# A graph network of two layers: transposes of x and the edges' counts moved to the end of the period ahead

## The chip, the cores and the metric

The kernel runs on one core of a Trainium2 chip. The metric is the device time of one execution in microseconds (us). A core has five engines with a queue each: TensorE (PE; its weight loads are listed apart as PEld), VectorE (DVE), ScalarE (ACT), GpSimd (POOL) and SyncE (SP), which here only issues DMA transfers. An engine takes its instructions in the order of the program, so an instruction that waits holds up all that stand behind it on the same engine.

## The reference

128 independent graphs of 128 nodes with 512 features in fp32. Each goes through a graph attention layer with 8 heads, a residual and a layer norm, and then through a hypergraph layer with a hidden width of 1024, again with residual and norm. Cut to what is computed:

```python
# layer 0
feats = einsum('bnf,hfu->bhnu', X, W)                    # 8 heads of 64
dense = leaky_relu(e_self[..., :, None] + e_neigh[..., None, :], 0.2) + NEG_BIG * (1 - A)
out = relu(einsum('bhij,bhju->bhiu', softmax(dense), feats) + b)
x = layernorm(x + out)
# layer 1
H = (adj != 0)
Dn = 1 / einsum('nce,ne->nc', H, adj[:, 0, :])           # 0 where the sum is not positive
Be = 1 / H.sum(axis=1)                                   # the edges' counts
conv(x, W, b) = Dn * (H @ (Be * (H.T @ (x @ W.T)))) + b
h = layer_norm(relu(conv(x, W1, b1))) * gamma + beta
y = conv(h, W2, b2)
x = layernorm(x + y)
```

## The kernel before

The graphs go two by two: a pair `p` has two graphs `g`, and there are 64 pairs. The work on one pair is spread over five periods of a software pipeline, so that in one period the stages of several pairs stand side by side. Every step is registered with a lag (in which period after the pair's own) and a time within the period. All steps of all pairs are sorted by `(p + lag) * T + time`, and the program is written in that order. The times only set the order on each engine; what an instruction waits for is data.

```python
    def at(lag, time, fn, *args, since=0, until=PAIRS):
        steps.append((lag, time, fn.__name__, range(since, until), fn, args))
# ... cut
    T = 38.6
# ... cut
            time += (p + lag) * T
            todo.append((first.get((name, p) + args, first.get((name, p), time)), run, (fn, p, args)))
    with tc.manual_schedule():
        for _, fn, args in sorted(todo, key=lambda e: e[0]):
            fn(*args)
```

The steps that the change touches. The rows of `x` are loaded a second time in blocks (`xb`), so that VectorE's 32x32 transposes give the whole transpose `xT`; the first layer's features are products of `xT` and of GpSimd's sums `xS` of its parts. The rows of `adj` are loaded in blocks (`ab`) too; their transpose gives `hT`, and its row sums the counts `deg`. `x_transpose`, `edges` and the loads:

```python
    def x_transpose(p, s, g):
        if g == 0:
            s["xT"] = work.tile([P, 2, KF, N], F32, tag="xT", name=f"xT_{p}")
        nc.vector.transpose(
            s["xT"][:, g].rearrange("p k (b n) -> p k b n", b=NB),
            s["xb"][:, g * NB:(g + 1) * NB].rearrange("p b (f k) -> p k b f", k=KF),
        )
    at(1, 4.7, x_transpose, 0, since=2)
    at(1, 5.3, x_transpose, 1, since=2)
# ... cut
    @step(1, 3.4)
    def edges(p, s):
        # ... cut: deg, hT
            nc.vector.transpose(hT.rearrange("p g (b n) -> p (g b) n", b=NB), s["ab"])
        for g in range(2):
            nc.vector.tensor_scalar(
                hT[:, g, :], src[:, g, :], 0.0, None, op0=ALU.not_equal, op1=ALU.add,
                accum_out=deg[:, g:g + 1],
            )
        nc.vector.tensor_scalar(deg, deg, 1.0, None, op0=ALU.max)
        nc.vector.reciprocal(deg, deg)
# ... cut
    @step(1, 10.8)   # scale_edges, VectorE: hB = hT * deg
    @step(1, 34.7)   # propagator, TensorE: pd = hB, hT
    @step(1, 35.8)   # r_evict, VectorE: R = pd * dnb
# ... cut: per pair
            todo.append((16.2 if p == 2 else p * T + 19.0, load_blocks, (p,)))
            todo.append((p * T + 28.5, load_edges, (p,)))
```

All of `xb`, `ab`, `xT` and `hT` have one buffer. Between the attention and the hidden layer stand, for the pair of lag 2, in the second half of the period:

```python
    # attended (VectorE): y = pav / row sums;  add_bias (GpSimd): y + b0
    at(2, 22.5, attended, 0)
    at(2, 27.9, attended, 1)
    at(2, 24.1, add_bias, 0)
    at(2, 29.2, add_bias, 1)
    def residual(p, s, g):
        y = s["y"][:, g, :]
        nc.vector.scalar_tensor_tensor(y, y, 0.0, s["x"][:, g, :], op0=ALU.max, op1=ALU.add)
        moments(p, s, "a", y, g)              # bn_stats, bn_aggr on VectorE
    at(2, 26.2, residual, 0)
    at(2, 30.7, residual, 1)
    at(2, 30.8, rstds, "a")                   # VectorE: + eps; GpSimd: power -0.5 -> rsa
    # ScalarE at 33.12 .. 33.14: sh = -mean * rsa, then y = y * rsa + sh
# ... cut
    at(3, 0.0, propagate, 0)                  # TensorE: pz from y and R
    at(3, 1.1, z_evict, 0)                    # ScalarE: zT = pz
    # hidden: products phX, phY, phW from zT and from GpSimd's sums zS; h_sum (VectorE), relu (ScalarE)
```

`masked` (GpSimd: `nb` + `neg`), `leaky` (ScalarE) and `largest` (VectorE: `nm`) of the pair of lag 1 stand around the period's end, and ScalarE's `leaky` of three half heads stands between `y` and `zT`. Attention's transposes `eT` (VectorE) stand ahead of the products `pav`, and the layer norm of the output `o` ahead of them.

The second layer's product with `W2` is a chain of seven products `pyX`, `pyY`, `pyW` in TensorE. VectorE adds two of them at a time to `y2`; a column more in the product, 1/DH times ones, carries the mean of `h`. Its deviation comes from the squares of `h`, which ScalarE forms and GpSimd folds, TensorE transposes (`pm`) and VectorE sums:

```python
        nc.scalar.activation(
            s["sq"][:, g, q * KH // 2:(q + 1) * KH // 2, :], hid(s, g, q), AF.Square
        )
# ... cut
    at(3, 31.3, y_sum, 0, 0, 0, "Y", until=LAST)
    at(3, 33.9, y_sum, 1, 1, 2, "W", until=LAST)
    at(4, 0.1, y_sum, 0, 1, 1, "W", until=LAST)
# ... cut
    @step(3, 36.0, until=LAST)
    def h_rstd(p, s):
        m2 = small.tile([P, 2], F32, tag="m2", name=f"m2_{p}")
        for g, m in enumerate((s["y2"][:, 0, 0, QU:], s["py", 1][:, QU:QU + 1])):
            nc.vector.tensor_tensor(m2[:, g:g + 1], m, m, op=ALU.mult)
        ve = small.tile([P, 2], F32, tag="ve", name=f"veh_{p}")
        nc.vector.tensor_reduce(
            ve, s["pm"][:, :2 * N].rearrange("p (g f) -> p g f", g=2), AX.X, ALU.add
        )
        nc.vector.scalar_tensor_tensor(
            ve, ve, 1.0 / DH, m2, op0=ALU.mult, op1=ALU.subtract
        )
        nc.vector.tensor_scalar(ve, ve, 0.0, EPS, op0=ALU.max, op1=ALU.add)
        s["rs", "h"] = small.tile([P, 2], F32, tag="rs", name=f"rsh_{p}")
        nc.gpsimd.tensor_tensor(s["rs", "h"], ve, mhalf, op=ALU.pow)
    # y_scale (VectorE, lag 4, 0.6 and 1.3): y2 * rsh + bw;  output (TensorE, 10.9): pq
```

`s["py", 1]` is a copy in SBUF that ScalarE makes of a product; `y2` lies in SBUF too.

Of the kernel before, what the change touches and what calls it, by code (L numbers as in the profile page):

```python
# [8 lines left out]
F32 = mybir.dt.float32  # L9
AF = mybir.ActivationFunctionType  # L10
ALU = mybir.AluOpType
AX = mybir.AxisListType

EPS = 1e-5
# [6 lines left out]
def kernel(  # L21
# [45 lines left out]
    nc = tc.nc  # L67
    G, N, F = x.shape
    P = 128
    DH = w1t.shape[1]  # L70
# [3 lines left out]
    KH = DH // P  # L74
    HALF = 512
    QU = HALF // 2
# [8 lines left out]
    small = ctx.enter_context(tc.tile_pool(name="small", bufs=4))  # L85
# [212 lines left out]
    LAST = PAIRS - 1  # L298
    steps = []

    def step(lag, time, since=0, until=PAIRS):

        def keep(fn):
            steps.append((lag, time, fn.__name__, range(since, until), fn, ()))
            return fn
        return keep

    def at(lag, time, fn, *args, since=0, until=PAIRS):
        steps.append((lag, time, fn.__name__, range(since, until), fn, args))
# [62 lines left out]
            s["xb"][:, g * NB:(g + 1) * NB].rearrange("p b (f k) -> p k b f", k=KF),  # L372
        )

    at(1, 4.7, x_transpose, 0, since=2)
    at(1, 5.3, x_transpose, 1, since=2)

    def x_transpose_first(p, s):
        s["px"] = [bank(f"px_{p}_{g}") for g in range(2)]
# [14 lines left out]
        for g in range(2):  # L394
            nc.tensor.transpose(s["pt"][:, g * N:(g + 1) * N], s["a"][:, g, :], ident)

    @step(1, 3.4)
    def edges(p, s):

        deg = small.tile([P, 2], F32, tag="deg", name=f"deg_{p}")  # L400
        hT = work.tile([P, 2, N], F32, tag="hT", name=f"hT_{p}")
        if p < 2:
            src = s["pt"][:, :2 * N].rearrange("p (g n) -> p g n", g=2)
        else:
            src = hT
# [8 lines that stand above are left out]
        s["hT"], s["be"] = hT, deg  # L414
# [65 lines left out]
    def feature(s, i, to, start):  # L480
# [4 lines left out]
          feature, FW, since=2)  # L485
# [315 lines left out]
    def hid(s, g, q):  # L801
        return s["h"][:, g, q * KH // 2:(q + 1) * KH // 2, :]
# [26 lines left out]
    def square(p, s, g, q):  # L829
        if (g, q) == (0, 0):  # L830
            s["sq"] = work.tile([P, 2, KH, N], F32, tag="sq", name=f"sq_{p}")
        nc.scalar.activation(
            s["sq"][:, g, q * KH // 2:(q + 1) * KH // 2, :], hid(s, g, q), AF.Square
        )

    for (g, q), t in (((0, 0), 13.5), ((0, 1), 15.9), ((1, 0), 19.4), ((1, 1), 21.2)):
        at(3, t, square, g, q)
# [21 lines left out]
    def weigh(s, i, to, start):  # L859
# [3 lines left out]
          QU, 1, until=LAST)  # L863
# [9 lines left out]
        else:  # L873
            nc.vector.tensor_tensor(dst, s["py", i][:, :n], s["py", where][:, :n], op=ALU.add)

    at(3, 31.3, y_sum, 0, 0, 0, "Y", until=LAST)
    at(3, 33.9, y_sum, 1, 1, 2, "W", until=LAST)
    at(4, 0.1, y_sum, 0, 1, 1, "W", until=LAST)
    at(3, 37.2, y_sum, 1, 0, None, "X", until=LAST)
# [2 lines left out]
    def sum_squares(p, s):  # L882
        s["pm"] = bank(f"pm_{p}")
        for g in range(2):
            nc.tensor.transpose(s["pm"][:, g * N:(g + 1) * N], s["sq"][:, g, 0, :], ident)

    @step(3, 36.0, until=LAST)
    def h_rstd(p, s):
        m2 = small.tile([P, 2], F32, tag="m2", name=f"m2_{p}")
        for g, m in enumerate((s["y2"][:, 0, 0, QU:], s["py", 1][:, QU:QU + 1])):  # L890
            nc.vector.tensor_tensor(m2[:, g:g + 1], m, m, op=ALU.mult)
        ve = small.tile([P, 2], F32, tag="ve", name=f"veh_{p}")
        nc.vector.tensor_reduce(
            ve, s["pm"][:, :2 * N].rearrange("p (g f) -> p g f", g=2), AX.X, ALU.add
        )
        nc.vector.scalar_tensor_tensor(
            ve, ve, 1.0 / DH, m2, op0=ALU.mult, op1=ALU.subtract
        )
        nc.vector.tensor_scalar(ve, ve, 0.0, EPS, op0=ALU.max, op1=ALU.add)
        s["rs", "h"] = small.tile([P, 2], F32, tag="rs", name=f"rsh_{p}")  # L900
        nc.gpsimd.tensor_tensor(s["rs", "h"], ve, mhalf, op=ALU.pow)

# [64 lines left out]
    def last_rstd(p, s, g, v):  # L967
        ve = small.tile([P, 1], F32, tag="ve", name=f"ve_{g}")
        nc.vector.tensor_scalar(ve, v, 0.0, EPS, op0=ALU.max, op1=ALU.add)
        rs = small.tile([P, 1], F32, tag="rs", name=f"rs_{g}")  # L970
        nc.gpsimd.tensor_tensor(rs, ve, mhalf[:, :1], op=ALU.pow)
        return rs

    def last_h_rstd(p, s, g):
        m = s["py", g, 0][:, QU:QU + 1]
        m2 = small.tile([P, 1], F32, tag="m2", name=f"m2_{g}")
        nc.scalar.activation(m2, m, AF.Square)
        v = small.tile([P, 1], F32, tag="vl", name=f"vl_{g}", bufs=2)
        nc.vector.tensor_reduce(v, s["pm", g][:, :N], AX.X, ALU.add)
        nc.vector.scalar_tensor_tensor(v, v, 1.0 / DH, m2, op0=ALU.mult, op1=ALU.subtract)  # L980
        s["rs", "h", g] = last_rstd(p, s, g, v)

    def last_scale(p, s, g, j):
# [37 lines left out]
    for t, fn, *args in (  # L1021
        (8.0, last_weights),
        (24.2, last_weigh, 0, 0), (27.8, last_weigh, 0, 1), (31.3, last_sum_squares, 0),
        (31.4, last_h_rstd, 0), (31.5, last_weigh, 1, 0), (32.5, last_scale, 0, 0),
        (32.6, last_scale, 0, 1), (34.9, last_sum_squares, 1), (35.0, last_h_rstd, 1),
        (35.1, last_output, 0, 0), (35.2, last_output, 0, 1), (35.3, last_weigh, 1, 1, (0,)),
        (35.5, last_o_sum, 0, 0), (35.6, last_scale, 1, 0), (36.0, last_o_sum, 0, 1),
        (36.5, last_o_rstd, 0), (37.0, last_output, 1, 0), (37.1, last_weigh, 1, 1, (1,)),
        (37.2, last_o_sum, 1, 0), (38.7, last_scale, 1, 1), (38.75, last_norm, 0),
        (38.9, last_output, 1, 1), (39.6, last_o_sum, 1, 1), (40.0, last_o_rstd, 1),  # L1030
        (40.5, last_norm, 1),
    ):
        at(3, t, fn, *args, since=LAST)


    T = 38.6
    todo = [
        (11.1, prepare_first, (0,)), (12.0, prepare_first, (1,)), (15.45, prepare_first_sums, ()),
        (12.1, load_weights, (nc.scalar, w2_blocks, w2t, DH // 2, QU)),
        (13.05, prepare_vectors, ()),  # L1040
        (14.05, load_weights, (nc.scalar, w1_blocks[:2], w1t, F // 2, HALF)),
        (12.95, load_first_row, (1,)),
        (15.46, load_weights, (nc.sync, w1_blocks[:1:-1], w1t, F // 2, HALF)),
        (16.1, everywhere, (b2_bc, b2, nc.sync)),
        (79.0, prepare_hidden, (nc.gpsimd, 2)), (79.1, prepare_hidden, (nc.gpsimd, 0)),
# [14 lines left out]
    first = {  # L1060
        ("spread_rows", 0): 13.5, ("neighbours", 0): 14.0,
        ("nodes", 0): 12.9, ("write_nodes", 0): 12.92, ("spread_nodes", 0): 15.9,
        ("edges", 0): 14.46, ("scale_edges", 0): 14.47, ("propagator", 0): 14.55,
        ("r_evict", 0): 99.76,
        ("spread_rows", 1): 15.72, ("nodes", 1): 15.55, ("write_nodes", 1): 15.85,
        ("edges", 1): 110.4, ("scale_edges", 1): 110.5, ("neighbours", 1): 80.1,
# [25 lines left out]
    for p in range(PAIRS):  # L1092
        if p > 1:
            todo.append(({2: 79.5, 3: 143.1}.get(p, p * T), load, (p,)))
            todo.append((16.2 if p == 2 else p * T + 19.0, load_blocks, (p,)))
            todo.append((p * T + 28.5, load_edges, (p,)))
        for lag, time, name, pairs, fn, args in steps:
            if p not in pairs:
                continue
            if p == 0 and lag == 2 and time < 8.5:  # L1100
                time *= 0.2
            if p == LAST:

                time = {
                    ("attend", 0): 24.25, ("attended", 0): 25.5, ("add_bias", 0): 25.6,
                    ("attend", 1): 25.95, ("attended", 1): 26.0, ("add_bias", 1): 26.1,
                    ("residual", 1): 26.3, ("rstds", "a"): 26.4,
                }.get((name,) + args[:1], time)
            if p == LAST - 1:
                time = {  # L1110
                    ("product", 2): 24.22 if (lag, time) > (3, 20.0) else time,
                    ("product", 5): 29.5 if (lag, time) > (3, 20.0) else time,
                    ("squares", 0): 26.5, ("squares", 1): 26.6, ("h_sums", 2): 22.3,
                    ("sum_squares",): 43.0, ("h_rstd",): 43.2, ("y_scale", 1): 5.8, ("y_scale", 0): 5.9,
                }.get((name,) + args[:1], time)
            time += (p + lag) * T
            todo.append((
                first.get((name, p) + args, first.get((name, p), time)), run, (fn, p, args)
            ))
# [46 lines left out]
```

## Time and profile before

| | before |
|---|---|
| time, median of 3 runs | 2584.59 us (2584.38 to 2586.65) |
| profiled run: span | 2570.0 us |
| TensorE matmul / weight loads busy | 2530.1 us (98%) / 2266.9 us (88%) |
| VectorE busy | 2114.2 us (82%) |
| GpSimd busy | 1753.4 us (68%) |
| ScalarE busy | 1535.0 us (60%) |
| TensorE clock granted | 0.997 |
| HBM traffic | 133 GB/s over the span |

A row of the profile's list in order of time reads: start in us, duration in us, engine, line of the kernel, operation, output and inputs by the program's names, shape, number of instructions merged; in brackets the idle time of the engine just before it, and the work whose end released it. A row of merged instructions has the sum, from the first start to the last end. On TensorE a weight load of the next product overlaps the matmul that runs.

### The profile page before, as it was taken

How to read it: one execution, taken by the hardware profiler on the slowest of the kernel's cores; microseconds unless marked ns; L12 is line 12 of the kernel's file. 1: busy time of each engine (PE TensorE's matmuls, PEld its weight loads, DVE VectorE, ACT ScalarE, POOL GpSimd, SP SyncE). 2: the span in 40 equal slices, each digit the busy share in tenths (PEclk: the TensorE clock that was granted, in tenths of full speed). 3: DMA queues.
4: the chain of work that ended last, by engine and by line, in shares of the span. 5: the costliest groups of instructions: out<-in, count | busy, mean ns of one | idle time of the engine just before them, and what ended most of it. 6: DMA issues, size and time to landing. Idle time of an engine off the chain costs nothing.

```text
span 2570.0 us, 48486 instructions
## 1 busy us (share of the span) xinstructions
PE 2530.1 (98%) x16349; PEld 2266.9 (88%) x16349; DVE 2114.2 (82%) x4584; ACT 1535.0 (60%) x4481; POOL 1753.4 (68%) x1806
## 2 busy tenths in 40 slices
PE   7999999999999999999999999999999999999998
PEld 5898988898888888989988889889888888898897
DVE  7887888878878878788888788787887888888875
ACT  4565665655755656557556566565565665655653
POOL 5767767676676676766766767667667666676674
PEclk9999999999999999999999999999999999999999
DMA  6444444444444444444454444444444444444431
GB/s 184 133 137 133 136 139 140 130 128 141 131 133 133 140 140 130 129 143 130 133 143 138 133 133 140 138 130 131 137 136 133 133 140 140 129 130 142 131 121 52
DMA packets 420840, 343.75 MB, mean 134 GB/s; under 512 B 141272, under 2 KB 370160, under 8 KB 420592
## 3 DMA queue, kind: packets, MB, share of 16 engines
q1 hardware_dynamic: 417120, 336.19, 44.2%
q10 hardware_dynamic: 3472, 4.47, 0.6%
q8 instruction: 130, 2.13, 0.3%
q14 instruction: 118, 0.97, 0.1%
HBM read 238.83 MB, written 101.71 MB: 133 GB/s over the span
## 4 chain that ended last, share of the span: by engine, by line
PE 83%; DVE 7%; DMA 4%; issue 2%; ACT 2%; POOL 1%; SPq 1%; DVEq 0%; POOLq 0%; ACTq 0%
PE phX L792 14%; PE pyX L473 14%; PE pfX L473 9%; PE phW L792 8%; PE pav L662 8%; PE pyW L473 7%; PE pfW L473 4%; PE pz L757 4%; PE phY L792 4%; PE pq L915 3%; PE pyY L473 3%; PE pfY L473 2%; DMA dnb<-dd_d 2%; ACT nb L592 1%; DVE o L745 1%
## 5 line engine op out<-in xcount | busy, mean ns | idle before, releaser
L329 ACT COPY py<-pyX 128x257 f32<-128x257 f32 x189 | 70.6, 374 | 539.4 <-PE pyX L473 526.3
L792 PEld LDWEIGHTS phX<-zS,w_sb 128*128 128x128 f32 x3072 | 363.1, 192 | 32.9 <-issue 29.3
L792 PE MATMUL phX<-zS,w_sb 128*128 128x128 f32 x3072 | 374.4, 275 | 2.1 <-POOL xS L455 1.3
L843 POOL TENSOR_TENSOR sq<-sq 128x512 f32<-128x512 f32 (+2 forms) x384 | 342.4, 892 | 20.2
L606 ACT ACTIVATE nb<-nb,nm 128x128 f32<-128x128 f32 x1024 | 324.5, 392 | 18.4 <-DVE nm L598 18.4
L576 POOL TENSOR_TENSOR nb<-nb,neg 128x512 f32<-128x512 f32 x256 | 317.8, 1273 | 14.3 <-DMA nb<-rd 14.3
L592 ACT ACTIVATE nb<-nb,ft 128x128 f32<-128x128 f32 x1020 | 317.3, 389 | 7.1 <-POOL nb L576 7.1
L822 ACT ACTIVATE h<-h,vecs 128x128 f32<-128x128 f32 x768 | 245.1, 392 | 88.3 <-DVE h L807 88.3
L693 DVE SCALAR_TENSOR_TENSOR y<-y,x 128x512 f32<-128x512 f32 x128 | 153.5, 1199 | 167.6 <-POOL y L686 167.6
L662 PEld LDWEIGHTS pav<-ft,eT 128*128 128x128 f32 x2048 | 243.5, 192 | 30.9 <-PE pfX L473 20.8
L709 POOL TENSOR_TENSOR rso<-veo,mhalf 128x2 f32<-128x2 f32 x63 | 44.1, 700 | 332.1 <-DVE veo L707 326.9
L662 PE MATMUL pav<-ft,eT 128*128 128x65 f32 x2048 | 246.8, 274 | 5.0
L473 PE MATMUL pyX<-w_sb,hS 128*128 128x257 f32 x1008 | 242.5, 382 | 0.0
L473 PE MATMUL pyX<-w_sb,h 128*128 128x257 f32 x1008 | 239.5, 379 | 0.5 <-ACT py L329 0.5
L473 PE MATMUL pyW<-w_sb,hS 128*128 128x256 f32 x1008 | 238.5, 378 | 0.0
L473 PEld LDWEIGHTS pyW<-w_sb,hS 128*128 128x128 f32 x1008 | 190.7, 189 | 27.4
L455 POOL TENSOR_TENSOR xS<-xT 128x256 f32<-128x256 f32 x124 | 117.9, 951 | 140.4 <-DVE xT L370 138.7
L473 PEld LDWEIGHTS pyX<-w_sb,h 128*128 128x128 f32 x1008 | 186.3, 190 | 25.5 <-ACT py L329 0.9
L473 PEld LDWEIGHTS pyX<-w_sb,hS 128*128 128x128 f32 x1008 | 186.2, 190 | 24.3
L686 POOL TENSOR_TENSOR y<-y,b_bc 128x512 f32<-128x512 f32 x128 | 162.4, 1269 | 62.9 <-DVE y L677 62.9
L598 DVE TENSOR_REDUCE nm<-nb 128x4 f32<-128x512 f32 x256 | 168.0, 676 | 2.9 <-ACT nb L592 2.2
L627 DVE STREAM_TRANSPOSE eT<-eb 128x512 f32<-128x512 f32 x252 | 161.9, 678 | 0.0
(167 smaller groups left out, 5865.1 us busy)
## 6 DMA issues: line engine op xcount, KB each, us to landing
nb<-rd SPq DMA_DIRECT2D x127, 512.0 KB, 6.3
ed<-nb SPq DMA_DIRECT2D x126, 512.0 KB, 2.6
eb<-ed SPq DMA_DIRECT2D x504, 128.0 KB, 2.9
x<-in_x_dram SPq DMA_DIRECT2D x64, 512.0 KB, 7.2
out_dram<-o SPq DMA_DIRECT2D x63, 512.0 KB, 2.8
xb<-in_x_dram SPq DMA_DIRECT2D x248, 128.0 KB, 3.0
a<-in_adj_dram SPq DMA_DIRECT2D x64, 128.0 KB, 6.5
w<-in_adj_dram SPq DMA_DIRECT2D x128, 64.0 KB, 4.3
```

The source lines that it names most:

```text
L473: nc.tensor.matmul(to[:, :n], lhs[:, k, :], rhs[:, k, :n], start=bool(start) and k == 0, stop=(k == nk - 1), skip_group_check=True,)
L576: nc.gpsimd.tensor_tensor(t, t, neg[:, :, None, :].to_broadcast([P, NB, HH, B]), op=ALU.add)
L592: nc.scalar.activation(t, t, AF.Prelu, bias=s["ft"][:, g, h, 0:1], alpha=SLOPE)
L598: nc.vector.tensor_reduce(s["nm"][:, g, hs], scores(p, s, g, hs).rearrange("p b h j -> p h b j"), AX.XY, ALU.max, negate=True,)
L606: nc.scalar.activation(t, t, AF.Exp, bias=s["nm"][:, g, h:h + 1])
L627: nc.vector.transpose(s["eT"][:, g, hs, :].rearrange("p h (b i) -> p h b i", b=NB), s["eb", g][:, :, hs, :].rearrange("p b h j -> p h b j"),)
L662: nc.tensor.matmul(t[:, h * (U + 1):(h + 1) * (U + 1)], s["eT"][:, g, q * HH + h, :], s["ft"][:, g, q * HH + h, 2:], start=True, stop=True,)
L686: nc.gpsimd.tensor_tensor(s["y"][:, g, :], s["y"][:, g, :], b0_bc, op=ALU.add)
L693: nc.vector.scalar_tensor_tensor(y, y, 0.0, s["x"][:, g, :], op0=ALU.max, op1=ALU.add)
L792: nc.tensor.matmul(to[:, m * N:(m + 1) * N], w[:, k, m * P:(m + 1) * P], rhs[:, k, :], start=bool(start) and m == 0 and k == 0, stop=(k == ...
L822: nc.scalar.activation(dst[:, k, :], src[:, k, :], AF.Relu, bias=b1_sb[:, c:c + 1])
L843: nc.gpsimd.tensor_tensor(t[:, :n, :], t[:, :n, :], t[:, n:2 * n, :], op=ALU.add)
```

## The change

VectorE's work is moved in the period and partly given to GpSimd.

- The two transposes of `x` are done 17 us sooner, in the second half of the pair's own period instead of early in the next one: one ahead of the first residual, one ahead of the second.
- The edges' transpose and counts are done at the end of the pair's own period, ahead of `R`. Their rows are loaded at 20.5 instead of 28.5, behind the blocks of `x`.
- The deviation of `h`: the squares of the two means are formed by GpSimd in a step of its own (`h_means`), and the subtraction, the floor at 0 and the epsilon by GpSimd as well. VectorE keeps the sum over `pm`. ScalarE's squares take the factor 1/DH with them, as a scale of DH^-0.5.
- The sum of `pyY` stands at 30.6 instead of 31.3, ahead of `h_means`, which reads its mean column.

It is meant to keep VectorE's queue short in the first part of a period and to use idle time in the second. Cut: the last pair's own deviation, which drops its factor 1/DH, and the starting times of pair 2.

```diff
-    at(1, 4.7, x_transpose, 0, since=2)
-    at(1, 5.3, x_transpose, 1, since=2)
+    at(0, 26.15, x_transpose, 0, since=2)
+    at(0, 30.65, x_transpose, 1, since=2)
...
-    @step(1, 3.4)
+    @step(0, 35.75)
     def edges(p, s):
...
         nc.scalar.activation(
-            s["sq"][:, g, q * KH // 2:(q + 1) * KH // 2, :], hid(s, g, q), AF.Square
+            s["sq"][:, g, q * KH // 2:(q + 1) * KH // 2, :], hid(s, g, q), AF.Square,
+            scale=DH ** -0.5,
         )
...
-    at(3, 31.3, y_sum, 0, 0, 0, "Y", until=LAST)
+    at(3, 30.6, y_sum, 0, 0, 0, "Y", until=LAST)
...
+    @step(3, 30.62, until=LAST)
+    def h_means(p, s):
+
+        s["m2"] = small.tile([P, 2], F32, tag="m2", name=f"m2_{p}")
+        for g, m in enumerate((s["y2"][:, 0, 0, QU:], s["py", 1][:, QU:QU + 1])):
+            nc.gpsimd.tensor_tensor(s["m2"][:, g:g + 1], m, m, op=ALU.mult)
+
     @step(3, 36.0, until=LAST)
     def h_rstd(p, s):
-        m2 = small.tile([P, 2], F32, tag="m2", name=f"m2_{p}")
-        for g, m in enumerate((s["y2"][:, 0, 0, QU:], s["py", 1][:, QU:QU + 1])):
-            nc.vector.tensor_tensor(m2[:, g:g + 1], m, m, op=ALU.mult)
...
-        nc.vector.scalar_tensor_tensor(
-            ve, ve, 1.0 / DH, m2, op0=ALU.mult, op1=ALU.subtract
-        )
-        nc.vector.tensor_scalar(ve, ve, 0.0, EPS, op0=ALU.max, op1=ALU.add)
+        nc.gpsimd.tensor_tensor(ve, ve, s["m2"], op=ALU.subtract)
+        nc.gpsimd.tensor_scalar(ve, ve, 0.0, EPS, op0=ALU.max, op1=ALU.add)
...
-            todo.append((p * T + 28.5, load_edges, (p,)))
+            todo.append((p * T + (28.5 if p == 2 else 20.5), load_edges, (p,)))
```

More of the change, by code (lines that the diff above doesn't have):

```diff
@@ L979, in last_h_rstd @@
         nc.vector.tensor_reduce(v, s["pm", g][:, :N], AX.X, ALU.add)
-        nc.vector.scalar_tensor_tensor(v, v, 1.0 / DH, m2, op0=ALU.mult, op1=ALU.subtract)
+        nc.vector.tensor_tensor(v, v, m2, op=ALU.subtract)
         s["rs", "h", g] = last_rstd(p, s, g, v)
@@ L1062 @@
         ("nodes", 0): 12.9, ("write_nodes", 0): 12.92, ("spread_nodes", 0): 15.9,
-        ("edges", 0): 14.46, ("scale_edges", 0): 14.47, ("propagator", 0): 14.55,
+        ("edges", 0): 14.46, ("edges", 2): 119.2,
+        ("x_transpose", 2, 0): 120.5, ("x_transpose", 2, 1): 121.1, ("scale_edges", 0): 14.47, ("propagator", 0): 14.55,
         ("r_evict", 0): 99.76,
```

## The prediction

> **What bounds the kernel now.** I read the busy table first, then TensorE's weight loads in order of time over several periods, then all engines over one period, and last the waits of single tiles.
>
> [...]
>
> TensorE has work in hand all the time, so the question is how often its weight loads pause. I took the start of each `pz` product (the first of a period) as the period's mark. From 135.47 to 2459.42 us there are 59 periods, on average 39.39 us: 2 of 38.7, 16 of 38.8 to 38.9, 30 of 39.4 to 39.5, 2 of about 40 and 9 of 40.2. The shortest, 38.66, has no flagged pause: that is TensorE's own length. The most common kind, in the weight-load rows:
>
> ```profile
> 1257.32 0.74 PEld L473 LDWEIGHTS pfX<-w_sb,xS 128*128 128x128 f32 x4 [0.42 <-POOL rso L709]
> 1260.35 1.86 PEld L662 LDWEIGHTS pav<-ft,eT 128*128 128x128 f32 x16 [0.51 <-PE pfX L473]
> 1278.40 1.97 PEld L757 LDWEIGHTS pz<-R,y 128*128 128x128 f32 x16
> ```
>
> Two pauses, 0.42 + 0.51 = 0.93 us. The names in brackets are only what ended last: the first waits for ScalarE's copy of `pfX`, the second for VectorE's transpose of `eT`. Both are late because VectorE is, one step earlier:
>
> ```profile
> 1245.25 2.12 DVE L370 STREAM_TRANSPOSE xT<-xb 128x512 f32<-128x512 f32 x2
> ...
> 1252.79 0.64 DVE L807 TENSOR_TENSOR h<-ph,phW 128x512 f32<-128x512 f32 x1
> ...
> 1253.47 1.28 ACT L822 ACTIVATE h<-h,vecs 128x128 f32<-128x128 f32 x4 [1.58 <-DVE h L807]
> ```
>
> VectorE works without a gap from the period's start through the edges' counts and both transposes of `x`; the sum `h` starts at 1252.79 although its last input, a ScalarE copy, ended at 1250.71. ScalarE waits 1.58 us for it. From there the lateness goes to the copy, to the layer norm of `o`, and to `eT`. The pauses are thus what VectorE's queue costs in the front of the period.
>
> The end of the period matters as much, because work moves there:
>
> ```profile
> 1269.29 1.90 PE L473 MATMUL pyY<-w_sb,h 128*128 128x257 f32 x8
> ...
> 1271.49 0.69 DVE L693 SCALAR_TENSOR_TENSOR y<-y,x 128x512 f32<-128x512 f32 x1 [1.38 <-POOL y L686]
> ...
> 1273.24 0.42 DVE L874 TENSOR_TENSOR y<-py,pyY 128x257 f32<-128x257 f32 x1
> ...
> 1273.41 0.70 POOL L709 TENSOR_TENSOR rsa<-vea,mhalf 128x2 f32<-128x2 f32 x1 [1.96 <-DVE vea L707]
> ...
> 1274.53 1.50 ACT L734 ACTIVATE y<-y,sh,rsa 128x512 f32<-128x512 f32 x2
> ...
> 1275.94 2.43 ACT L592 ACTIVATE nb<-nb,ft 128x128 f32<-128x128 f32 x8
> ...
> 1278.28 0.35 ACT L872 COPY y<-pyX 128x256 f32<-128x256 f32 x1
> ...
> 1278.53 1.28 ACT L592 ACTIVATE nb<-nb,ft 128x128 f32<-128x128 f32 x4
> ...
> 1279.71 0.58 ACT L769 COPY zT<-pz 128x512 f32<-128x512 f32 x1
> ```
>
> This is a chain without slack: second residual (L693), moments, `rsa`, then ScalarE without a gap from `y` to `zT`; `zT` ends at 1280.29 and the `phX` product that reads it loads its first weights at 1280.34. From residual to `phX` is 8.85 us, and in 58 of these periods it is 8.84 to 8.89. It has no slack: in the period before 176.07 the residual was 9.01 us ahead, and ScalarE then reached `zT` just as `pz` was done; at 8.85 it is at work up to that very moment. So whatever delays this residual against TensorE delays TensorE by as much.
>
> **What the Trainium skill says.** "Perfetto Trace Analysis", section "Identifying the Most-Contended Engine": [...]weight loads are the better measure[...]. The trace agrees: 98% of matmul time hides the pauses that the 88% row shows. "GPSIMD Engine Reference", section "Specifications": GpSimd shares its SBUF interfaces with VectorE, and contends with instructions with two SBUF inputs. The trace agrees: the residual takes 1.74 us at 1266.35 beside GpSimd's sums of squares and 0.69 us at 1271.49 with GpSimd idle. The same page's section "Engine selection" gives small elementwise work to VectorE; here VectorE is the queue that is too long, so the advice is rightly turned round if GpSimd has room there. "Vector Engine (DVE) Microarchitecture Reference", section 3.8, says a transpose sustains one element per cycle and lane: `eT` takes 0.67 us for 512 elements and `xT` 1.09 for as many. So the `xT` figure is taken from the trace, not from the page.
>
> **The change part by part.** *Front of the period.* VectorE loses two `xT` transposes (2.06 us start to start) and the edges' counts (1243.66 to 1245.25, 1.6 us), 3.7 us. Then `h` is held by ScalarE's copy instead of the queue: about 1.9 us earlier. This removes the pauses at `pfX` and `pav`, and the 0.85 us at `phW` of the 40.2 kind: 39.39 - 38.66 = 0.73 us per period, 43 us over 59 periods.
>
> *h_rstd.* VectorE gives up four small steps, by their rows 0.64 + 0.29 + 0.68 + 0.48 = 2.1 us, and keeps the reduction. GpSimd gains four. No row has their cost there; between a memset of 128x2 (0.10 us) and the power (0.70 us) I estimate 0.2 each. The chain to `y_scale` gets longer, but `pq`, which needs it, comes 9 us later. Worth nothing on the path.
>
> *First transpose*, at 26.15: VectorE idles 1.35 us there for GpSimd's bias sum. 1.05 us fit, if `xb` has landed. It is issued after `o`, which comes about 1 us sooner. Worth 0.
>
> *Edges at 35.75*: 1.7 us, followed by `R` 0.42. Counted below from a later start, `R` still ends about 1 us ahead of `pz`. Worth 0.
>
> *Second transpose and the sum of `pyY`*, at 30.65 and 30.6. This is the step on which I stake the number. The build's order on VectorE is: second `attended`, sum of `pyY`, transpose, residual. Before, the sum stood after the residual. Now the residual can't start before `pyY` is done, plus a sum, plus a transpose. In the unpaused period after 137.41, `phX` being 0, `pyY` starts to load at 27.40 and, as above (1269.08 to 1271.19), ends 2.11 later: 29.51. Wake-up 0.11, sum 0.34 to the next start, transpose 1.03: the residual starts at 30.99. Add 8.85: the next `phX` is at 39.84. TensorE alone would have been there at 38.66, so it stands still 1.2 us before `phX` in every period.
>
> *Sum.* The new period is 39.84 against 39.39: the front gives 0.73 and the end takes 1.18. 0.45 x 59 = 27 us on 2570; on the timed 2584.59 this is 2611. The timed runs are 13 us longer than the profiled one; if that is more of the 40.2 kind, there is more to win there, so I shade to 2608.
>
> **The rivals.** *(a) No new wait.* If the residual had slack, or the sum did not hold it, the pauses just vanish: 2584.6 - 43 = 2541, 1.7% faster. For it: 0.7 us per period is truly idle. Against it: the constant 8.85, and an order that is fixed. It can't pass 2% by much even if all goes well. *(b) Transfers take over.* The edges' rows (1024 pieces of 128 bytes) now stand ahead of the `rd` write and the `nb` read in the same queue. Masking may start about 33.6 after `phX`; I put `nb`'s landing at 32 to 33 (issue at about 26, 6.3 us to land). If `rd` waits 2 us more, the period passes 40.3 and the time 2636. For it: less than 1 us of slack. Against it: `nb` no longer shares its landing with `ab`. *(c) GpSimd is the bound:* four small steps of 0.7 us would add 1.5 us ahead of its `zS` sums, where it waits about 1 us now; some 0.5 us per period, near 2630.
>
> **Range and chances.** The main line is +0.9%. A residual that has 0.3 us of slack after all gives 2590, later transfers or slow small steps 2630. I take 2608 with 2580 to 2632; faster by over 2% 0.04, within 2% 0.84, slower by over 2% 0.12.
>
> **What would show it.** Right: no pause at `pfX`, `pav` and `phW`; about 1.2 us before `phX`, released by ScalarE's `zT`; VectorE idle about 1.3 us before the sum of `pyY`; GpSimd no longer waiting for `xT` (138.7 us now); a period of 39.8, nearly constant. Wrong: a period of 38.7 with no pause at `phX`, or a residual that starts less than 1 us after `pyY`'s end; or GpSimd's masking released by `nb`'s landing.

## The result and the profile after

| | before | after |
|---|---|---|
| time, median | 2584.49 us (2581.56 to 2586.65, 4 runs) | 2596.41 us (2596.01 to 2596.96, 4 runs) |
| profiled run: span | 2570.0 us | 2594.2 us |
| VectorE busy | 2114.2 us | 1915.8 us |
| GpSimd busy | 1753.4 us | 1833.0 us |
| period, mean of 59 | 39.39 us (38.66 to 40.23) | 39.78 us (39.76 to 39.79) |

The kernel before has one run more here than above. The ratio is 1.0047, with a 95% interval of 1.003 to 1.0064: slower, by 12 us. VectorE has 198 us less to do and the kernel takes longer. First TensorE's weight loads of one period of the changed kernel, from the list in order of time, as they were shown for the kernel before:

```profile
1212.35 1.86 PEld L792 LDWEIGHTS phX<-zT,w_sb 128*128 128x128 f32 x16 [1.09 <-ACT zT L769]
...
1228.26 0.83 PEld L473 LDWEIGHTS pfX<-w_sb,xS 128*128 128x128 f32 x4
...
1230.91 1.98 PEld L662 LDWEIGHTS pav<-ft,eT 128*128 128x128 f32 x16
...
1249.08 1.97 PEld L757 LDWEIGHTS pz<-R,y 128*128 128x128 f32 x16
...
1252.13 1.86 PEld L792 LDWEIGHTS phX<-zT,w_sb 128*128 128x128 f32 x16 [1.09 <-ACT zT L769]
```

No bracket at `pfX` and `pav`: both pauses of the front are gone. In their place stands one of 1.07 to 1.09 us before `phX`, released by ScalarE's `zT`, in each of the 59 periods. The period from `phX` to `phX`, each taken at its first weight load, is 1252.13 - 1212.35 = 39.78; below, "after `phX`" counts from that load. What holds `zT` is seen at the end of the same period, over all engines:

```profile
1239.97 1.90 PE L473 MATMUL pyY<-w_sb,h 128*128 128x257 f32 x8
1240.00 1.27 POOL L686 TENSOR_TENSOR y<-y,b_bc 128x512 f32<-128x512 f32 x1 [0.98 <-DVE y L677]
...
1241.97 0.42 DVE L876 TENSOR_TENSOR y<-py,pyY 128x257 f32<-128x257 f32 x1 [2.05 <-PE pyY L473]
1242.31 1.09 DVE L370 STREAM_TRANSPOSE xT<-xb 128x512 f32<-128x512 f32 x1
...
1243.33 0.65 DVE L693 SCALAR_TENSOR_TENSOR y<-y,x 128x512 f32<-128x512 f32 x1
...
1245.21 0.70 POOL L709 TENSOR_TENSOR rsa<-vea,mhalf 128x2 f32<-128x2 f32 x1 [2.40 <-DVE vea L707]
```

The second residual (L693) has its input at 1241.27, when GpSimd's bias sum (L686) ends. It starts at 1243.33. In between VectorE waits for `pyY`, which ends at 1241.87 and whose sum now stands first, and then does the transpose. The bracket of 2.05 us at the sum is VectorE's idle time. From the residual to the next `phX` is 1252.13 - 1243.33 = 8.80 us, close to the 8.85 of the kernel before.

### The profile page after: what moved, and what is told of

It reads as the page before. It is cut to its first block, busy times and chain, and to the rows that moved or that the text cites. A ratio compares the mean times of both kernels' runs of the same rounds, so it can differ in the third digit from the quotient of the medians.

```text
span 2594.2 us, 48549 instructions
## 1 busy us (share of the span) xinstructions
PE 2513.1 (97%) x16349; PEld 2272.8 (88%) x16349; DVE 1915.8 (74%) x4332; ACT 1537.0 (59%) x4481; POOL 1833.0 (71%) x2058
## 4 chain that ended last, share of the span: by engine, by line
PE 68%; ACT 13%; DMA 7%; issue 6%; DVE 2%; POOL 2%; SPq 1%; DVEq 0%; POOLq 0%; ACTq 0%
PE phX L792 18%; PE phW L792 9%; PE pfX L473 8%; ACT nb L592 8%; PE pav L662 7%; PE pyX L473 6%; DMA x<-in_x_dram 6%; PE phY L792 4%; PE pq L919 4%; PE pfW L473 4%; PE pyY L473 3%; PE pfY L473 2%; ACT y L734 2%; POOL rsa L709 1%; ACT zT L769 1%
## 5 line engine op out<-in xcount | busy, mean ns | idle before, releaser
L598 DVE TENSOR_REDUCE nm<-nb 128x4 f32<-128x512 f32 x256 | 174.6, 683 | 116.0 <-ACT nb L592 56.4
L822 ACT ACTIVATE h<-h,vecs 128x128 f32<-128x128 f32 x768 | 238.5, 392 | 2.2 <-DVE h L807 2.2
L686 POOL TENSOR_TENSOR y<-y,b_bc 128x512 f32<-128x512 f32 x128 | 162.8, 1272 | 70.9 <-DVE y L677 70.9
L792 PE MATMUL phX<-zT,w_sb 128*128 128x128 f32 x1024 | 132.7, 283 | 56.3 <-ACT zT L769 56.3
L329 ACT COPY ph<-phX 128x512 f32<-128x512 f32 x192 | 112.5, 586 | 118.1 <-PE phX L792 118.1
L792 PEld LDWEIGHTS phX<-zT,w_sb 128*128 128x128 f32 x1024 | 120.7, 194 | 68.1 <-ACT zT L769 68.0
```

What stands on the lines that cost most here:

```text
L329: nc.scalar.copy(t[:, :n], s[kind, "X"][:, :n])
L598: nc.vector.tensor_reduce(s["nm"][:, g, hs], scores(p, s, g, hs).rearrange("p b h j -> p h b j"), AX.XY, ALU.max, negate=True,)
L686: nc.gpsimd.tensor_tensor(s["y"][:, g, :], s["y"][:, g, :], b0_bc, op=ALU.add)
L792: nc.tensor.matmul(to[:, m * N:(m + 1) * N], w[:, k, m * P:(m + 1) * P], rhs[:, k, :], start=bool(start) and m == 0 and k == 0, stop=(k == ...
L822: nc.scalar.activation(dst[:, k, :], src[:, k, :], AF.Relu, bias=b1_sb[:, c:c + 1])
```

## The experiments

**e1, the sum behind the residual.** The changed kernel, with `y_sum` where it was and `h_means` moved with it:

```diff
-    at(3, 30.6, y_sum, 0, 0, 0, "Y", until=LAST)
+    at(3, 31.3, y_sum, 0, 0, 0, "Y", until=LAST)
-    @step(3, 30.62, until=LAST)
+    @step(3, 35.9, until=LAST)
     def h_means(p, s):
```

> The changed kernel with the sum of pyY back behind the second residual (31.3) and the squares of the means behind the masking (35.9). Theory (the sum, held by pyY, and the transpose behind it delay the second residual, and through ScalarE's gapless chain phX): the residual starts when GpSimd's bias sum is done, about 28.97 us after phX instead of 30.98; no pause before phX; period 38.66 instead of 39.78, so 59 x 1.12 = 66 us less: about 2530 us. Rival (the transposes and counts themselves, at the end of the period, are what costs: their collisions with GpSimd, or R late): the period stays over 39.3, over 2565 us.

Measured: 2530.86 us (2530.26 to 2532.17) against 2574.88 of the kernel before beside it, ratio 0.9832 (0.9819 to 0.9846). The period is 38.67. The rows of one period of e1, whose `phX` is at 1259.35:

```profile
1286.83 1.11 DVE L370 STREAM_TRANSPOSE xT<-xb 128x512 f32<-128x512 f32 x1
1286.96 1.90 PE L473 MATMUL pyY<-w_sb,h 128*128 128x257 f32 x8
1286.99 1.26 POOL L686 TENSOR_TENSOR y<-y,b_bc 128x512 f32<-128x512 f32 x1 [0.98 <-DVE y L677]
...
1288.29 0.69 DVE L693 SCALAR_TENSOR_TENSOR y<-y,x 128x512 f32<-128x512 f32 x1 [0.35 <-POOL y L686]
...
1290.04 0.42 DVE L876 TENSOR_TENSOR y<-py,pyY 128x257 f32<-128x257 f32 x1
```

The transpose now lies wholly in the time in which GpSimd adds the bias, and VectorE is even idle for 0.35 us after it. The residual starts 1288.29 - 1259.35 = 28.94 after `phX`. Neither the transposes nor the counts cost anything at the end of the period; the order does. The next `phX` comes 9.73 us after the residual, 0.9 more than in the changed kernel: here the chain to `zT` has time to spare.

**e2, the transpose behind the residual.** The sum stays first; only the transpose is taken out of its way.

```diff
-    at(0, 30.65, x_transpose, 1, since=2)
+    at(0, 33.0, x_transpose, 1, since=2)
```

> The changed kernel with the second transpose of x behind the second residual (33.0 instead of 30.65); the sum of pyY stays ahead. Theory (both the wait for pyY and the transpose behind it count in full): the residual starts 29.96 after phX (pyY's end 29.51, wake-up 0.11, sum 0.34), 1.03 sooner than in the changed kernel; phX at 29.96 + 8.8 = 38.76, period 38.7 to 38.8, about 2535 us. Rival (the wait for pyY alone is the cost, the transpose slips into its shadow): no gain, about 2596 us.

Measured: 2538.28 us (2537.9 to 2540.6), ratio 0.9862 (0.9848 to 0.9875). The period is 38.79 in 58 of the periods. One of them, whose first `phX` is at 1224.83:

```profile
1252.44 1.90 PE L473 MATMUL pyY<-w_sb,h 128*128 128x257 f32 x8
...
1254.44 0.42 DVE L876 TENSOR_TENSOR y<-py,pyY 128x257 f32<-128x257 f32 x1 [2.08 <-PE pyY L473]
1254.79 0.68 DVE L693 SCALAR_TENSOR_TENSOR y<-y,x 128x512 f32<-128x512 f32 x1
...
1256.53 1.10 DVE L370 STREAM_TRANSPOSE xT<-xb 128x512 f32<-128x512 f32 x1
...
1263.62 1.86 PEld L792 LDWEIGHTS phX<-zT,w_sb 128*128 128x128 f32 x16
```

The residual starts 29.96 after `phX`, between e1's 28.94 and the changed kernel's 30.98. So at the residual the wait with its sum (1.02) and the transpose (1.02) both count in full, one after the other. In the period they do not weigh the same. The wait mostly uses up what the chain had to spare in e1: 29.96 + 8.83 = 38.79, and the period grows by 0.12. The transpose behind it then adds 0.99 of its 1.02. GpSimd's two squares, which e1 moved along with the sum, stay early here, so they are not what costs.

**e3, the early sum alone.** The kernel before with `y_sum` at 30.6.

```diff
-    at(3, 31.3, y_sum, 0, 0, 0, "Y", until=LAST)
+    at(3, 30.6, y_sum, 0, 0, 0, "Y", until=LAST)
```

> The kernel before with nothing but the sum of pyY at 30.6 instead of 31.3. Theory: without a transpose behind it the sum delays the residual from 30.60 to 30.75 in a period of 39.45, 0.15 us and no more; 59 x 0.15 = 9 us, about 2593 us. Rival (the early sum alone costs what the change lost, 1.1 us): about 2650 us.

Measured: 2592.2 us (2590.0 to 2593.86), ratio 1.0069 (1.0056 to 1.0081). The number was met, but against 2574.88 beside it that is 17 us and not 9. In the trace the residual starts at 30.76 in the median period, as expected (30.75). But the mix of periods moved as well: 21 of 40.2 us here, against 9 in the profile before; the mean period is 39.75. No period of 38.85 is left: GpSimd's `zS` sums start 0.80 after `phX` instead of 0.92, and even a `y_scale` that starts at 0.17 runs into them (see e4). The rival's 1.1 us per period is excluded.

**e4, the deviation alone.** The kernel before with the small steps on GpSimd, nothing moved:

```diff
+    @step(3, 35.9, until=LAST)
+    def h_means(p, s):                   # ... cut: GpSimd's squares of the means, as in the change
# ... cut: the same squares on VectorE go, and ScalarE's squares take the scale
-        nc.vector.scalar_tensor_tensor(ve, ve, 1.0 / DH, m2, op0=ALU.mult, op1=ALU.subtract)
-        nc.vector.tensor_scalar(ve, ve, 0.0, EPS, op0=ALU.max, op1=ALU.add)
+        nc.gpsimd.tensor_tensor(ve, ve, s["m2"], op=ALU.subtract)
+        nc.gpsimd.tensor_scalar(ve, ve, 0.0, EPS, op0=ALU.max, op1=ALU.add)
```

> The kernel before with nothing but the deviation's small steps on GpSimd (squares of the means at 35.9, behind the masking). Theory: 2.1 us leave VectorE, but y_scale then waits for GpSimd's power, which comes as late as VectorE did; y_scale starts at about 0.4 after phX as before, and the period does not move: within 5 us of before, about 2584 us. Rival (VectorE's total load is the bound): 59 x up to 1 us less, about 2530 to 2550 us.

Measured: 2565.22 us (2564.63 to 2569.08), ratio 0.9967 (0.9955 to 0.9978), 10 us faster; the expectation of no change failed. `y_scale` does start at 0.40 after `phX` in the median, against 0.37 before. But it ends sooner. In the kernel before, in a period of 38.85, in one of 39.45 and in one of 40.2:

```profile
1202.19 1.40 DVE L905 SCALAR_TENSOR_TENSOR y<-y,rsh,bw_bc 128x512 f32<-128x512 f32 x2
...
1202.96 1.22 POOL L780 TENSOR_TENSOR zS<-zT 128x256 f32<-128x256 f32 x1 [1.05 <-ACT zT L769]
...
1241.26 1.88 DVE L905 SCALAR_TENSOR_TENSOR y<-y,rsh,bw_bc 128x512 f32<-128x512 f32 x2
...
1241.82 0.78 POOL L780 TENSOR_TENSOR zS<-zT 128x256 f32<-128x256 f32 x1 [0.86 <-ACT zT L769]
...
1397.78 2.42 DVE L905 SCALAR_TENSOR_TENSOR y<-y,rsh,bw_bc 128x512 f32<-128x512 f32 x2
1397.80 0.72 POOL L780 TENSOR_TENSOR zS<-zT 128x256 f32<-128x256 f32 x1 [0.32 <-ACT zT L769]
```

and in e4:

```profile
1276.74 1.55 DVE L908 SCALAR_TENSOR_TENSOR y<-y,rsh,bw_bc 128x512 f32<-128x512 f32 x2 [1.26 <-POOL rsh L904]
...
1277.72 1.16 POOL L780 TENSOR_TENSOR zS<-zT 128x256 f32<-128x256 f32 x1
```

`y_scale` is two instructions; where nothing holds the second, it starts 0.66 us after the first. Where a `zS` sum already runs when the second comes, the pair takes 1.88 us; where the first meets a sum too (here that sum starts 0.02 us later), 2.42. Where both of VectorE's come first, the pair takes 1.40 to 1.56 and the `zS` sum is the one that is stretched, to 1.22 or 1.16 against 0.73 by itself. In e4 GpSimd comes to `zS` at 1.39 after `phX` instead of 0.92, after its new steps and the mask, and the pair takes 1.55 or 1.56 in 59 of 63 periods. So the gain looks like a collision avoided, and not like work removed. No run takes away the collision alone; for it speaks that the period goes with the end of `y_scale` after `phX`: 1.55 and 38.85, 1.96 and 39.27 (e4), 2.25 and 39.43, 3.34 and 40.22.

**e5, the moves alone.** As e1, but with the deviation left on VectorE (the two transposes, the counts and their load as in the change, `y_sum` at 31.3, all else as in the kernel before).

> The kernel before with the moves alone: both transposes, the edges' counts and their earlier load as in the change, the sum of pyY left at 31.3 and the deviation left on VectorE. Theory (the moves are the whole gain, and they bring the period down to TensorE's own 38.66; the deviation's steps add nothing once the front has room): as the version with the sum behind the residual, 2531 us, within 5 us. Rival (the deviation's move is needed to make room for the counts at the period's end): y_scale or R comes too late, a pause before pz or phX, over 2540 us.

Measured: 2531.4 us (2531.01 to 2531.72), ratio 0.9819 (0.9806 to 0.9833); the period is 38.67. With the front free, the deviation's move adds nothing. Nor does the collision cost anything there: the `y_scale` pair takes 1.88 us or more in 13 of 60 periods, and these are as long as the others.

**e6, the edges' rows late.** e1 with the load of the edges' rows as before.

```diff
-            todo.append((p * T + (28.5 if p == 2 else 20.5), load_edges, (p,)))
+            todo.append((p * T + 28.5, load_edges, (p,)))
```

> The version with the sum behind the residual, but the edges' rows loaded at 28.5 as before, behind nb and dnb in the queue. Theory (the counts now stand ahead of R on VectorE, so their rows have to be there by 33.5 after phX; issued as late as before they land at about 35 to 36.5): R and with it pz wait 1 to 2 us, period 39.7 to 40.6, 2595 to 2640 us. Rival (the load's time is not on the path): 2531 us.

Measured: 2561.79 us (2560.2 to 2565.34), ratio 0.9939 (0.9924 to 0.9955), mean period 39.13. That is 31 us over e1, half of the least that was expected, and in another place. The waits of e6 and some rows of its time list:

```profile
DVE hT L406 <- DMA ab<-in_adj_dram: 139.0, 56, 4.0
```
```profile
1271.74 0.45 DVE L406 STREAM_TRANSPOSE hT<-ab 128x256 f32<-128x256 f32 x1 [2.89 <-DMA ab<-in_adj_dram]
...
1272.07 1.97 PEld L757 LDWEIGHTS pz<-R,y 128*128 128x128 f32 x16
...
1273.08 0.40 DVE L437 TENSOR_TENSOR R<-pd,dnb 128x256 f32<-128x256 f32 x1
...
1278.29 1.86 PEld L792 LDWEIGHTS phX<-zS,w_sb 128*128 128x128 f32 x16 [0.63 <-POOL zS L780]
```

VectorE waits for the rows, 139 us in 56 periods (total, times, longest). But `pz` does not wait: in this period it loads at 1272.07, while `R` is only made at 1273.08. `R` has three buffers, and what is made here is read by the `pz` after the next (lag 1 and lag 3); I had tied it to the next. What TensorE feels is what stands behind on VectorE: the sum over `pm`, with it GpSimd's deviation steps, and so `y_scale` and `zS`, for whose sums the next `phX` product pauses by 0.3 to 1.5 us in 33 steady periods, 0.63 here.

**e7 and e8, both kernels again, side by side** (no edit).

> The changed kernel once more, beside these runs. Its period is set by one chain of fixed steps, so it should repeat: 2594 to 2598 us, 59 periods of 39.78. If the kernel before then stands at 2575 and not at 2584, the difference is 21 us, near the 24 us between the two profiled spans, and the smaller 12 us was the kernel before's own scatter.

> The kernel before once more, with a profile of its own. If the kinds of its periods (38.85, 39.45, 40.2) come from whether y_scale collides with GpSimd's zS sums, their mix differs from run to run and the span with it, between about 2565 and 2590 us, each span being the sum of its kinds. If the mix is fixed, 2570 again with the same counts.

Measured: the changed kernel 2598.18 us (2597.3 to 2598.65), at the upper edge of what was expected, again with every steady period at 39.77 to 39.79; the kernel before 2577.57 (2575.02 to 2582.73, 12 runs) as e8, and 2578.66 (2570.79 to 2583.21, 17 runs) beside it. Ratio of e7 1.0078 (1.0065 to 1.0091): 20 us here. e8's profile has 20 steady periods of 38.8 to 38.9, 24 of 39.4 to 39.5 and 14 of 40.2, where the first profile has 16, 30 and 9 of 40.2; its span is 2573.4 instead of 2570.0. In both profiles the kind follows from the start of `y_scale` after `phX` without an exception: up to 0.17 it is 38.9 or less, between 0.34 and 0.40 it is 39.4 to 39.5, and from 0.90 on it is 40.2, with `y_scale` ending at 3.32 or later (two of 39.9 start at 0.89 and end at 2.78). So by these profiles the kernel before scatters by which collision it falls into, and the changed one, with one fixed chain, does not.

## Why the prediction was right

*What bounds the kernel before: right.* VectorE's queue in the front of the period made the pauses. With its 3.7 us moved away (e1, e5) the period is TensorE's own, 38.67 against the 38.66 read from the trace. No run moves the transposes without the counts, so what each is worth stays open. GpSimd's wait for `xT`, 138.7 us before, is 3.9 after.

*The chain without slack: right for both kernels.* It takes 8.85 us from residual to `phX` before and 8.80 after, and in e2, where residual and chain come to 38.79, the period is 38.79 against 38.67. It is not so in every order: in e1 the chain has 0.9 us to spare.

*The second transpose and the sum: right*, and to the hundredth. Expected start of the residual 30.99, measured 30.98; expected period 39.84, measured 39.78, the rest being the 0.05 of the 8.85. e1 and e2 split the 2.04 us of delay (28.94, 29.96, 30.98): 1.02 for the sum and its wait, 1.02 for the transpose. One sign was misread: VectorE is idle for 2.05 us before the sum, not 1.3. About 1.3 is the wait for GpSimd's bias sum, and `pyY` ends 0.6 us after that.

*h_rstd worth nothing on the path: right in the changed kernel* (e5 against e1), *wrong for the kernel before*, where it is worth 10 us (e4), by the traces through the collision. Four steps of 0.2 us were estimated; the groups of the changed kernel show 200, 202, 198 and 223 ns.

*Edges: right in worth, wrong in reason.* I measured `R` against the next `pz`; it has a period more to spare (e6).

*The first transpose: worth 0, right.* It waits for `xb` in 27 periods, 14.0 us in all, and the pauses show none of it.

*The rivals.* (a) is what e1 makes: it takes 44 us less than the kernel before beside it, where 43 were forecast for the front, so that gain is real and was more than given back by the order. (b) and (c) did not come about: in the changed kernel no masking waits for `nb` in the steady periods, and GpSimd's small steps took 0.2 us each and not 0.7: with them on either engine the kernel takes the same time (e1, e5). The 2630 given for (c) is not its own sum: 0.5 x 59 on 2608 is 2638.

*The size: too large.* 2608 was forecast, 2596.4 measured; +23 against +12. The term of the sum that was mis-sized is the period before, 39.39, which came from one profile. The spans did grow by 24 us, as the sum said. But the timed runs of the kernel before beside it took 2584.5, 13 us longer than its profiled one (2571.8), and the changed kernel's were within 1 us of its own. 13 us over 59 periods are 0.22 each, so the period of those runs was about 39.6, an estimate. I shaded by 3 us for this. Beside the experiments the kernel before moves between 2571 and 2583 from run to run, and three of the four runs beside the result (2584.4 to 2586.7) lie above all 39 of these. More periods of 40.2 would make such a time, but no trace of those runs exists; the cause stays open.

## What to carry to other kernels

Before work is moved into another instruction's idle time, ask what stands next to it in the same queue: a sum placed 0.7 us earlier in the program, ahead of the data it waits for, turned idle time that the transpose would have filled into a delay of 2 us at the residual, of which 1.1 us reached the period. Look for the chain that runs from one engine to the next without a gap, and measure its length in many periods; if it is constant to a few hundredths, every further delay at its head counts in full in that order of the program. In another order it can have time to spare, as in e1. And when a pipelined kernel's period takes a few distinct values, look for a collision that some periods have and others don't, and don't take the mean of one profile as its time.

The best version here is e1 or e5, at 2531 us: 1.7 to 1.8% faster than the kernel before, with no pause at TensorE's weight loads in the steady periods but one of 0.39 us in e1.

## What the runs showed of the hardware

Where VectorE's `y_scale`, with two inputs from SBUF, met GpSimd's `zS` sums, the one that came first kept nearly its own pace: a `y_scale` pair took 1.40 us and the `zS` sum behind it 1.22 instead of 0.73 (1202.19 and 1202.96), or the pair took 1.88 and the sum 0.78 (1241.26 and 1241.82). The Trainium skill, "GPSIMD Engine Reference", section "Specifications", states that GpSimd shares its SBUF interfaces with VectorE and contends with instructions that have two SBUF inputs; the traces agree and show what it costs here. In the kernel before, where the first `zS` sum comes 0.92 after `phX`, a difference of 0.2 us in the start of `y_scale` (0.15 or 0.37) decided which of the two it was, and with it 0.6 us of the period. It is the order of the two and not the start by itself: in e3, where the sum comes at 0.80, the pair took 1.90 us from a start at 0.17. The transposes of `x` have one input and were hardly stretched: in the changed kernel one took 1.12 us beside GpSimd's sums of squares (1236.04) and one 1.09 with hardly any of GpSimd's work beside it (1242.31). And the small subtraction, 128x2, took VectorE 0.80 us beside GpSimd's masking (1238.80) and 0.16 with GpSimd idle (1395.96), 0.79 in the median; on GpSimd it took 0.20.
